# The opening of a two-layer graph-attention kernel: transfers in order of use, folds by vector, a first softmax by tile, and norms placed anew

## The chip, the cores and the metric

The kernel runs on one core of one Trainium2 chip. The core has a matrix engine (TensorE, PE in the profile), a vector engine (VectorE, DVE), an activation engine (ScalarE, ACT), a general engine (GpSimd, POOL) and a queue engine (SyncE, SP). Transfers between the chip's memory and the core's own can be issued from SP, ACT and POOL. The metric is the device time in microseconds (us) of one execution, the median of several.

## What is computed

The input x has 128 graphs of 64 nodes with 512 features each, 8192 rows of 512 numbers, all float32. One adjacency matrix of 64 x 64 serves all graphs.

```python
h = maximum(layernorm(x), 0)                        # "norm1" in the kernel
def gat(x, W, a):                                   # per head: W is [F, O], a is [2*O]
    Wh = x @ W
    f1, f2 = Wh @ a[:O], Wh @ a[O:]
    e = f1[:, None] + f2[None, :]                   # scores, 64 x 64 per graph
    e = where(e > 0, e, 0.01 * e)
    e = where(adj > 0, e, -1e9)
    return softmax(e, -1) @ Wh
h = elu(gat over 4 heads, 512 features each)        # concatenated to 2048 features
out = elu(gat(h, W_out, a_out))                     # one head
ffn = maximum(out @ w1 + b1, 0) @ w2 + b2
result = x + layernorm(ffn + out) * gamma + beta
```

## The kernel before

The 8192 rows are 64 tiles of 128 rows (two graphs each), worked in 16 groups of four tiles. The scores of the first layer don't need `x @ W`: the kernel first *folds* the vectors into the weights (`wa = W @ a`), multiplies the normalised tiles with the folded columns (`pf`), spreads these numbers into sums of pairs (`s1pe`), takes the softmax (`s1e`, `s1A`), transposes the weights of the softmax (`s1pt`, `at`), mixes the nodes (`pz`, `z`), and only then multiplies by the heads' matrices (`g_a`). Matrix products of 512 x 512 are done with seven instead of eight block products, so there are sums of blocks around them (`zs`, on DVE for the first head and on POOL later; `hS`, `h` on POOL).

Loads and the four head matrices. `nc.sync` issues from SP, `nc.scalar` from ACT, `nc.gpsimd` from POOL:

```python
    X[0] = load(0)                                  # 256 KB, from SP
    aj = const.tile([P, N], mybir.dt.int32, name="aj")
    for b in range(NB):
        nc.sync.dma_start(out=aj[ts(b, N), :], in_=adj)
    ar = ...                                        # the vectors, 8 rows of 512
    nc.sync.dma_start(out=ar, ...)
    for t in range(1, G):
        X[t] = load(t)
    ah = ...                                        # the vectors, 32 rows of 128
    nc.sync.dma_start(out=ah, ...)
    # ... (cut)
    def fetch(m):                                   # matrix m, 1 MB
        MT[m] = big.tile([P, KC, O], FP, tag=homes[m], name=f"pw{m}")
        queue = nc.scalar if m < H else nc.gpsimd
        queue.dma_start(out=MT[m], in_=mats[m].rearrange("(k p) o -> p k o", p=P))
```

The fold. Three matrices are folded on DVE: each vector is spread over the partitions by PE into a PSUM bank (`pab`, two banks for each matrix, one for each half `c` of the vector), then each of four blocks `k` of the matrix is multiplied with it and summed along the row (`jk`). The third matrix is folded on PE: transposes (`pwt`), a copy by ACT (`wT`), and products with the vectors (`pwa`).

```python
    def fold_dve(m, ab):
        for k in range(KC):
            for c in range(2):
                junk = wk.tile([P, O], FP, tag="t", name=f"jk{c}_{m}_{k}")
                nc.vector.scalar_tensor_tensor(
                    junk, MT[m][:, k, :], 1.0, ab[c], ALU.mult, ALU.mult,
                    accum_out=wa[:, k, c * H + m:c * H + m + 1],
                )
```

The norm of a tile: statistics on DVE, two steps on POOL, the activation on ACT. A tile of the third or a later group has its statistics wait for the last matrix product written down before it (`LAST["pe"]`), so that DVE doesn't wait for a late x in front of urgent work:

```python
    def norm_stats(src, tag, t):
        st = sm.tile([P, 6], FP, tag=tag + "st", name=f"{tag}st{t}")
        ins = nc.vector.bn_stats(st, src)
        if tag == "n1" and t >= 2 * G:
            tc.add_manual_dep(ins.ins, LAST["pe"].ins.name, ...)
        # ... bn_aggr, + eps on DVE (n1mv, n1ve); power -0.5 on POOL (n1rs)

    def norm1(t):
        # ... norm_stats; POOL: nb = -mean * rstd (n1nb)
        nc.scalar.activation(HN[t], X.pop(t), AF.Relu, bias=nb, scale=rstd)
        # ... POOL: sums of half tiles (hns) for two of four tiles
```

The softmax of two tiles with four heads (`q == 8`, 128 x 512 numbers):

```python
        nc.vector.tensor_tensor(e, pe, mask, ALU.add)
        # ... (f1 is not None: the second layer)
        nc.vector.scalar_tensor_tensor(e, e, ALPHA, e, ALU.mult, ALU.max)
        nc.vector.tensor_reduce(mx, e, AX.X, ALU.max)
        nc.vector.tensor_tensor(e, e, mx[:, :, None].to_broadcast([P, q, N]), ALU.subtract)
        nc.scalar.activation(e, e, AF.Exp)
        nc.vector.tensor_reduce(s, e, AX.X, ALU.add)
        nc.vector.reciprocal(r, s)
        nc.vector.tensor_tensor(A[:, :, 0:H], e, r, ALU.mult)      # shapes cut
        LAST["A"] = nc.vector.tensor_copy(A[:, :, H], A[:, :, 0])  # first head again, as a fifth
```

The opening and the first group:

```python
    for m in range(H):
        fetch(m)
    masks()                                         # small constants on DVE
    for t in range(G):
        norm1(t)
    ab = {m: spread_a(m) for m in (0, 1)}
    aT = turn_a()                                   # transposes ah (pah)
    fold_dve(0, ab[0])
    fold_dve(1, ab[1])
    fold_pe(2, aT)
    for t in range(G):
        transpose_h(t)                              # pth, copied by ACT to hT
    fold_dve(3, spread_a(3))
    for m in range(H):
        weight_sums(m, LAST["nb"])                  # POOL: sums of blocks (pt), stored (tc)
    project_f(0)                                    # pf, then L on ACT, U and R on DVE
    scores1(0)                                      # s1pe
    for p in range(2):
        attn_weights(p)                             # softmax of tiles 0 and 1, of 2 and 3
    transpose_weights(0)
    attn = attend1(0)                               # pz, copied to z by ACT and DVE
    for fn in attn[:2]:
        fn()
    head0 = project1(0, 0)                          # the first products, g_a
    # ... (cut)
        attn = attend1(g + 1) if g + 1 < NG else []
        norms, scores, turns = stage_a(g + 2)
        # ... (cut)
        first = mix(attn, tr, [nothing] * len(attn))
        # ... (cut)
        if g == 0:
            run(project2(g), first + early + norms + scores + turns + [...])
```

`run(steps, side)` writes down the steps of a product (`g_b`) and, between them, in even distance, the steps of the list `side`. `early` are the block sums of the next group.

Of the kernel before, what the change touches and what calls it, by code (L numbers as in the profile page):

```python
# [11 lines left out]
ALU = mybir.AluOpType  # L12
# [10 lines left out]
def gat_preln_kernel(  # L23
# [72 lines left out]
        return tl  # L96

    X[0] = load(0)
    aj = const.tile([P, N], mybir.dt.int32, name="aj")
    for b in range(NB):  # L100
        nc.sync.dma_start(out=aj[ts(b, N), :], in_=adj)
    ar = wk.tile([2 * H, O], FP, tag="elu", name="ar", bufs=3)
    nc.sync.dma_start(out=ar, in_=a_heads.rearrange("h (r p) -> (h r) p", p=O))
    for t in range(1, G):
        X[t] = load(t)
    ah = wk.tile([2 * H * KC, P], FP, tag="elu", name="ah", bufs=3)
    nc.sync.dma_start(out=ah, in_=a_heads.rearrange("h (r p) -> (h r) p", p=P))

    negm = const.tile([P, N], FP, name="negm")
    blkones = const.tile([P, NB, N], FP, name="blkones")  # L110
# [35 lines left out]

    def fetch(m):
        MT[m] = big.tile([P, KC, O], FP, tag=homes[m], name=f"pw{m}")
        queue = nc.scalar if m < H else nc.gpsimd
        queue.dma_start(out=MT[m], in_=mats[m].rearrange("(k p) o -> p k o", p=P))  # L150

    def spread_a(m):
# [19 lines left out]

    def fold_dve(m, ab):

        for k in range(KC):
            for c in range(2):
                junk = wk.tile([P, O], FP, tag="t", name=f"jk{c}_{m}_{k}")
                nc.vector.scalar_tensor_tensor(
                    junk, MT[m][:, k, :], 1.0, ab[c], ALU.mult, ALU.mult,
                    accum_out=wa[:, k, c * H + m:c * H + m + 1],  # L180
                )
# [69 lines left out]
    def run(steps, side=()):  # L251

        side, done = list(side), 0
        for i, fn in enumerate(steps):
            fn()
            while done * len(steps) < (i + 1) * len(side):
                side[done]()
                done += 1
# [81 lines left out]
    def norm_stats(src, tag, t):  # L340


        st = sm.tile([P, 6], FP, tag=tag + "st", name=f"{tag}st{t}")
        ins = nc.vector.bn_stats(st, src)  # L344
        if tag == "n1" and t >= 2 * G:
            tc.add_manual_dep(
                ins.ins, LAST["pe"].ins.name,
                mybir.DependencyInfo(mybir.DependencyClass.Sync, mybir.DependencyReason.DATA),
                reason="x may come late: not in front of what is urgent",
            )  # L350
        mv = sm.tile([P, 2], FP, tag=tag + "mv", name=f"{tag}mv{t}")
        nc.vector.bn_aggr(mv, st)
        ve = sm.tile([P, 1], FP, tag=tag + "ve", name=f"{tag}ve{t}")
        nc.vector.tensor_scalar(ve, mv[:, 1:2], EPS, None, ALU.add)
        rstd = sm.tile([P, 1], FP, tag=tag + "rs", name=f"{tag}rs{t}")
        nc.gpsimd.tensor_tensor(rstd, ve, mhalf, ALU.pow)
        return mv[:, 0:1], rstd
# [62 lines left out]
    def softmax(pe, f1, q, tag, t):  # L420


        w = "s1" if q == 8 else "s2"
        e = sm.tile([P, q, N], FP, tag=w + "e", name=f"{tag}e{t}", bufs=1)
        mask = negm[:, None, :].to_broadcast([P, q, N])
        if f1 is None:
            nc.vector.tensor_tensor(e, pe, mask, ALU.add)
        else:
            nc.vector.tensor_tensor(e, pe, f1[:, :, None].to_broadcast([P, q, N]), ALU.add)
            nc.vector.tensor_tensor(e, e, mask, ALU.add)  # L430
        nc.vector.scalar_tensor_tensor(e, e, ALPHA, e, ALU.mult, ALU.max)
        mx = sm.tile([P, q], FP, tag=w + "mx", name=f"{tag}mx{t}")
        nc.vector.tensor_reduce(mx, e, AX.X, ALU.max)
        nc.vector.tensor_tensor(e, e, mx[:, :, None].to_broadcast([P, q, N]), ALU.subtract)
        nc.scalar.activation(e, e, AF.Exp)
        s = sm.tile([P, q], FP, tag=w + "s", name=f"{tag}s{t}")
        nc.vector.tensor_reduce(s, e, AX.X, ALU.add)
        r = sm.tile([P, q], FP, tag=w + "r", name=f"{tag}r{t}")
        nc.vector.reciprocal(r, s)
        if q == 8:  # L440
            A = sm.tile([P, 2, H + 1, N], FP, tag=w + "A", name=f"{tag}A{t}", bufs=1)
            nc.vector.tensor_tensor(
                A[:, :, 0:H], e.rearrange("p (t h) m -> p t h m", h=H),
                r.rearrange("p (t h) -> p t h", h=H)[:, :, :, None].to_broadcast([P, 2, H, N]), ALU.mult,
            )
            LAST["A"] = nc.vector.tensor_copy(A[:, :, H], A[:, :, 0])
            return A

        rb = sm.tile([P, q, NB], FP, tag=w + "rb", name=f"{tag}rb{t}")
        nc.vector.tensor_tensor(  # L450
            rb,
            blkones[:, :, 0][:, None, :].to_broadcast([P, q, NB]),
            r[:, :, None].to_broadcast([P, q, NB]),
            ALU.mult,
        )
        A = sm.tile([P, q, NB, N], FP, tag=w + "A", name=f"{tag}A{t}", bufs=1)
        nc.vector.tensor_tensor(
            A,
            e[:, :, None, :].to_broadcast([P, q, NB, N]),
            rb[:, :, :, None].to_broadcast([P, q, NB, N]),  # L460
            ALU.mult,
        )
        return A
# [156 lines left out]
    def project2(g):  # L620
        slot = {1: "11", 2: "12", 3: "12", 4: "22", 5: "S1", 6: "11", 7: "S1"}
        h1 = dict(H1)
        wh = big.tile([P, G, FO], FP, tag="wh2", name=f"wh2_{g}")
        WH2[g] = wh

        def post(what, a, b=None, to=None):
            behind = {"s1": ("11", "S1", "11"), "s5": ("S1", "22", "11"), "c11": ("12", "12", "11")}
            if what in behind:
                dst, x0, x1 = (h1[n] for n in behind[what])
                for h in range(H):  # L630
                    nc.gpsimd.tensor_tensor(dst[:, h], x0[:, h], x1[:, h], ALU.subtract)  # L631
            if what[0] != "c":
                return
            r, c = quadrant(what)
            dst = wh[:, 2 * r:2 * r + 2, c * Q:(c + 1) * Q]
            if b is None:
                nc.scalar.copy(dst, a)  # L637
            else:
                nc.vector.tensor_tensor(dst, a, b, ALU.add)

        ms = [H + h for h in range(H)]
        return unit(
            f"b{g}", product_n(ms, lambda p, i: h1[slot[p]][:, i]), post, (1, 5, 6, 2, 7, 3, 4)
        )
# [147 lines left out]
        return [fn for _, _, fn in sorted(keyed, key=lambda k: k[:2])]  # L792


    for m in range(H):
        fetch(m)
    masks()
    for t in range(G):
# [47 lines left out]
    for g in range(NG):  # L846
        if g >= 1:
            side = stage_e(g - 1)
        else:
            side = sum(stage_a(1), [])  # L850
            for i, m in ((5, 4), (9, 5), (12, 6), (17, 7)):
                side.insert(i, lambda m=m: more_sums(m))
        done, n = 0, 6 * H
        for i in range(n):
            if i % 6 == 0:
                steps = head0 if (g, i) == (0, 0) else project1(g, i // 6)
            if (g, i // 2) != (0, 0):
                steps[i % 6]()
            while done * n < (i + 1) * len(side):
                side[done]()  # L860
                done += 1
        flush_late()
        attn = attend1(g + 1) if g + 1 < NG else []
        norms, scores, turns = stage_a(g + 2)
        tr, ff, fin = feed_forward(g - 1) if g >= 1 else ([], [], [])
        if g == NG - 1:
            run(project2(g), tr + [nothing] * 6 + ff[:2])
            run(ff[2:], [
                lambda: [scores2(g, j) for j in range(G)], lambda: spread2(g), nothing, nothing,
                lambda: softmax2(g), *[nothing] * 7, lambda: transpose_weights2(g), nothing,  # L870
                *[lambda q=q: attend2(g, q) for q in range(2)], nothing,
            ])
            continue
        early = [lambda: z_sums(g + 1, 0)]
        first = mix(attn, tr, [nothing] * len(attn))
        if g >= 1:
            first[5:5] = norms[:1]
            first[10:10] = norms[1:]
        if g == 0:
            def sums_late(m):  # L880
                fetch(m)
                weight_sums(m, LAST["A"])

            run(project2(g), first + early + norms + scores + turns + [
                load_rows, lambda: sums_late(M1), lambda: sums_late(M2)
            ])
        else:
            run(project2(g), first + mix(
                ff[:7] + early + ff[7:12] + fin[:1] + ff[12:13] + fin[1:2] + ff[13:],
                scores + [nothing] * 8,  # L890
            ) + mix(fin[2:], [nothing] + turns + [nothing] * 2))
# [32 lines left out]
```

## Time and profile before

| what | value |
|---|---|
| device time, median of 3 executions | 2320.34 us (2318.64 to 2320.38) |
| span of the profiled execution | 2318.7 us |
| granted clock of PE, mean | 0.995 of full speed |
| moved by transfers | 366.40 MB, 158 GB/s on the mean |
| start of the first head product `g_a` | 55.80 us |

In the profile a line such as `PE 2279.8 (98%)` gives the time an engine was busy, its share of the span, and the number of its instructions. PEld is PE's loading of weights, which runs beside its products. A matrix product of float32 shows as two records. A tile's name stands without its number (`pw` is any of `pw0` to `pw3`), and L158 is line 158 of the kernel. A wait is put down to the operation that came last before the waiting one started. The page's second part has the span in 40 equal slices of 58 us, one digit each, in tenths of the slice.

### The profile page before, as it was taken

Reading aid. Unit: us, or ns where it says so; the run is one execution under the profiler, and the core shown is the slowest. Engines: PE = TensorE matmul, PEld = TensorE weight load, DVE = VectorE, ACT = ScalarE, POOL = GpSimd, SP = SyncE. Lnnn points to the kernel's source line nnn. Section 1 sums busy time; section 2 is a strip of 40 time slices with the busy share of each in tenths; the row PEclk is TensorE's granted clock in tenths of the full one; section 3 lists DMA queues with packets and bytes.
Section 4 is the critical chain, followed back from the end, with each engine's and each line's share of the span. In section 5 each row is a group of like instructions: output and inputs, shape, how many; then the busy total and the mean of one; then the engine's idle time right before and its main releaser. Section 6 shows DMA issues by size and latency. Waiting matters only on the chain. (4 is left out here: it accounts for less than half of the span.)

```text
span 2318.7 us, 33446 instructions
## 1 busy us (share of the span) xinstructions
PE 2279.8 (98%) x11933; PEld 1922.7 (83%) x11933; DVE 1272.2 (55%) x2210; ACT 905.5 (39%) x1623; POOL 1029.9 (44%) x917
## 2 busy tenths in 40 slices
PE   6999999999999999999999999999999999999997
PEld 4878888888888888888888888888888888888885
DVE  6635465555646555465555646555464654744427
ACT  2534425153352534425254252533525244251512
POOL 6664544425344352444425444253443525533324
PEclk8999999999999999999999999999999999999999
DMA  8545464554545445454454545445453454635543
GB/s 296 174 171 195 133 183 135 157 161 133 183 135 176 131 147 178 133 182 132 151 171 133 182 135 162 150 140 182 132 179 131 147 180 128 182 119 168 163 146 104
DMA packets 259571, 366.40 MB, mean 158 GB/s; under 512 B 24232, under 2 KB 147144, under 8 KB 259408
## 3 DMA queue, kind: packets, MB, share of 16 engines
q1 hardware_dynamic: 252784, 343.31, 47.3%
q0 software_dynamic: 4512, 16.78, 2.0%
q10 hardware_dynamic: 2112, 4.19, 0.5%
q8 instruction: 96, 1.57, 0.3%
q14 instruction: 67, 0.55, 0.1%
HBM read 336.92 MB, written 27.26 MB: 157 GB/s over the span
## 5 line engine op out<-in xcount | busy, mean ns | idle before, releaser
L322 PE MATMUL g_b<-w,h 128*128 128x256 f32 x2560 | 592.5, 379 | 0.0
L322 PEld LDWEIGHTS g_b<-w,h 128*128 128x128 f32 x2560 | 481.4, 190 | 63.7 <-issue 0.9
L307 PE MATMUL g_a<-z,w 128*128 128x256 f32 x1520 | 360.9, 380 | 0.7 <-DVE g_a L597 0.7
L307 PE MATMUL g_a<-zs_z,w 128*128 128x256 f32 x1504 | 350.9, 381 | 0.0
L307 PEld LDWEIGHTS g_a<-zs_z,w 128*128 128x128 f32 x1504 | 282.0, 190 | 60.8 <-issue 24.3
L307 PEld LDWEIGHTS g_a<-z,w 128*128 128x128 f32 x1520 | 287.2, 190 | 45.0 <-DVE g_a L597 6.1
L601 POOL TENSOR_TENSOR hS<-hS,h 128x512 f32<-128x512 f32 x64 | 83.1, 1299 | 354.8 <-DVE hS L565 354.8
L322 PE MATMUL g_b<-w,hS 128*128 128x256 f32 x1024 | 238.5, 379 | 0.0
L563 ACT ACTIVATE exc<-g_a 128x512 f32<-128x512 f32 x256 | 152.1, 594 | 179.0 <-DVE g_a L597 106.7
L565 DVE SCALAR_TENSOR_TENSOR h<-exc,g_a 128x512 f32<-128x512 f32 x192 | 131.7, 686 | 157.3 <-ACT exc L564 156.2
L322 PEld LDWEIGHTS g_b<-w,hS 128*128 128x128 f32 x1024 | 192.1, 190 | 25.8 <-issue 1.0
L564 ACT ACTIVATE exc<-exc 128x512 f32<-128x512 f32 x256 | 161.5, 631 | 7.0
L631 POOL TENSOR_TENSOR h<-h,h 128x512 f32<-128x512 f32 x64 | 86.8, 1364 | 135.3 <-PE g_b L322 135.3
L631 POOL TENSOR_TENSOR h<-hS,h 128x512 f32<-128x512 f32 x64 | 81.2, 1270 | 142.5 <-PE g_b L322 142.5
L481 ACT COPY at<-s1pt 128x512 f32<-128x512 f32 x64 | 34.7, 588 | 279.8 <-PE s1pt L479 279.8
L332 POOL TENSOR_TENSOR zs_z<-zS,z 128x512 f32<-128x512 f32 x63 | 89.0, 1414 | 122.6 <-PE g_a L307 118.6
L773 POOL TENSOR_TENSOR xr<-xr,bs 128x512 f32<-128x512 f32 x64 | 96.1, 1502 | 72.6 <-DMA xr<-in_x_dram 58.4
L307 PE MATMUL g_c<-ot,w 128*128 128x256 f32 x512 | 122.8, 383 | 1.4 <-DVE ot L735 1.4
L322 PE MATMUL g_d<-w,rt 128*128 128x256 f32 x512 | 121.5, 380 | 2.2 <-DVE o L765 1.5
L307 PE MATMUL g_a<-zS,w 128*128 128x256 f32 x496 | 117.2, 379 | 0.0
L655 DVE SCALAR_TENSOR_TENSOR jf<-wh,ao 128x512 f32<-128x512 f32 x128 | 99.0, 811 | 31.8 <-ACT wh L637 31.6
L333 POOL TENSOR_TENSOR zs_z<-z,zs_z 128x512 f32<-128x512 f32 x63 | 85.1, 1351 | 61.8 <-PE g_a L307 39.1
(159 smaller groups left out, 3485.8 us busy)
## 6 DMA issues: line engine op xcount, KB each, us to landing
w<-tc SPq DMA_DIRECT2D x632, 256.0 KB, 2.7
w<-in_L_gnn_W_heads_dram SPq DMA_DIRECT2D x192, 256.0 KB, 3.0
w<-in_L_gnn_W_out_dram SPq DMA_DIRECT2D x192, 256.0 KB, 2.7
w<-in_L_gnn_w_dram SPq DMA_DIRECT2D x96, 256.0 KB, 2.7
x<-in_x_dram SPq DMA_DIRECT2D x64, 256.0 KB, 3.8
xr<-in_x_dram SPq DMA_DIRECT2D x128, 128.0 KB, 2.7
out_dram<-o SPq DMA_DIRECT2D x128, 128.0 KB, 2.4
tc<-pt POOLq DMA_DIRECT2D x20, 512.0 KB, 4.2
```

The source lines that it names most:

```text
L307: LAST["pe"] = nc.tensor.matmul(bk[:, o, :], w[:, k, ts(o, P)], a[:, k, :], start=start and o == 0 and k == 0, stop=k == 1, skip_group_che ...
L322: LAST["pe"] = nc.tensor.matmul(bk[:, j, :], a[:, k, ts(j, P)], w[:, k, :], start=start and k == 0 and j == 0, stop=i == len(ms) - 1 and k ...
L332: eng.tensor_tensor(s2, s1, a11, ALU.subtract)
L333: eng.tensor_tensor(s4, a12, s2, ALU.subtract)
L481: nc.scalar.copy(AT[t].rearrange("p b h n -> p (b h) n"), pt)
L563: nc.scalar.activation(ex, src, AF.Relu, scale=-1.0)
L564: nc.scalar.activation(ex, ex, AF.Exp, scale=-1.0)
L565: nc.vector.scalar_tensor_tensor(dst, ex, -1.0, src, ALU.add, ALU.max)
L601: nc.gpsimd.tensor_tensor(dst, dst, H1["22"][:, h], ALU.add)
L631: nc.gpsimd.tensor_tensor(dst[:, h], x0[:, h], x1[:, h], ALU.subtract)
L655: nc.vector.scalar_tensor_tensor(junk, WH2[g][:, j], 1.0, ao[:, c, :], ALU.mult, ALU.mult, accum_out=f[:, c, j:j + 1],)
L773: nc.gpsimd.tensor_tensor(xr, xr, bs, ALU.add)
```

## The change

It concerns the opening and the first two groups alone, and it has four parts.

1. *Transfers in order of use over three queues.* adj and `ah` go to POOL's queue; SP brings x0, `ar`, x1 to x3 and then the matrices 1 and 3; ACT brings the matrices 0 and 2 and has no more to issue. This is to have the first tiles and the third matrix early, and ACT free.
2. *Fold by vector.* The two loops of the fold change places: all four blocks with the first half of the vector, then with the second. The first bank of the vector is free sooner, and half of a fold can begin before the second half is spread.
3. *First softmax tile by tile.* The softmax of tiles 0 and 1 is done as two of 128 x 256, the second beginning after the first's subtraction. The first tile's transposes can start before the second's weights are there.
4. *Norms of the second and third group placed anew.* The statistics of the second group (`t >= G`) now wait for a matrix product too, which takes them out of the stretch before the first scores. The norms of the third group stand between the steps that mix the nodes of the second, and no more behind all of them and the next block sums.

```diff
     X[0] = load(0)
-    aj = const.tile([P, N], mybir.dt.int32, name="aj")
-    for b in range(NB):
-        nc.sync.dma_start(out=aj[ts(b, N), :], in_=adj)
     ar = wk.tile([2 * H, O], FP, tag="elu", name="ar", bufs=3)
     nc.sync.dma_start(out=ar, in_=a_heads.rearrange("h (r p) -> (h r) p", p=O))
     for t in range(1, G):
         X[t] = load(t)
     ah = wk.tile([2 * H * KC, P], FP, tag="elu", name="ah", bufs=3)
-    nc.sync.dma_start(out=ah, in_=a_heads.rearrange("h (r p) -> (h r) p", p=P))
+    nc.gpsimd.dma_start(out=ah, in_=a_heads.rearrange("h (r p) -> (h r) p", p=P))
+    aj = const.tile([P, N], mybir.dt.int32, name="aj")
+    for b in range(NB):
+        nc.gpsimd.dma_start(out=aj[ts(b, N), :], in_=adj)
 ...
-        queue = nc.scalar if m < H else nc.gpsimd
+        queue = nc.scalar if m in (0, 2) else nc.sync if m < H else nc.gpsimd
 ...
-        for k in range(KC):
-            for c in range(2):
+        for c in range(2):
+            for k in range(KC):
 ...
-        if tag == "n1" and t >= 2 * G:
+        if tag == "n1" and t >= G:
 ...
+        n = H if w == "s1" and t == 0 else q
+        for i in range(0, q, n):
+            ei, mi, si, ri = e[:, i:i + n], mx[:, i:i + n], s[:, i:i + n], r[:, i:i + n]
+            mask = negm[:, None, :].to_broadcast([P, n, N])
+            if f1 is None:
+                ins = nc.vector.tensor_tensor(ei, pe[:, i:i + n], mask, ALU.add)
+                if i:
+                    tc.add_manual_dep(ins.ins, ahead.ins.name, ...)   # one tile after the other
+            ...
+            nc.vector.scalar_tensor_tensor(ei, ei, ALPHA, ei, ALU.mult, ALU.max)
+            nc.vector.tensor_reduce(mi, ei, AX.X, ALU.max)
+            ahead = nc.vector.tensor_tensor(ei, ei, mi[:, :, None].to_broadcast([P, n, N]), ALU.subtract)
+            nc.scalar.activation(ei, ei, AF.Exp)
+            nc.vector.tensor_reduce(si, ei, AX.X, ALU.add)
+            nc.vector.reciprocal(ri, si)
+            if q == 8:
+                ...   # product and copy of the first head, for the tiles of this part
 ...
-    for m in range(H):
+    for m in (0, 2, 1, 3):
         fetch(m)
 ...
-            run(project2(g), first + early + norms + scores + turns + [
+            mixed = attn[:2] + norms[:1] + attn[2:] + norms[1:] + [nothing] * 4
+            run(project2(g), mixed + early + scores + turns + [
```

## The prediction

> **What bounds the kernel now.** I read the page first, then stretches of the span, then TensorE's waits, then the order of time. The page says that TensorE (PE) is the bound almost everywhere, and that only the first of the 40 slices is thin:
>
> ```profile
> PE 2279.8 (98%) x11933; PEld 1922.7 (83%) x11933; DVE 1272.2 (55%) x2210; ACT 905.5 (39%) x1623; POOL 1029.9 (44%) x917
> ...
> PE   6999999999999999999999999999999999999997
> ```
>
> Busy PE is not PE at its peak, but here no engine keeps it waiting in the middle, as the stretches show (busy us and instruction counts per engine, granted clock, DMA share, GB/s):
>
> ```profile
> 0.00:66.00 66.00, 46.88 (x221) 33.65 (x221) 39.64 (x113) 22.05 (x38) 36.05 (x53) 0.90 0.78 273
> 66.00:116.00 50.00, 49.74 (x282) 42.85 (x283) 32.78 (x44) 26.46 (x49) 37.60 (x34) 1.00 0.57 185
> 116.00:184.00 68.00, 64.69 (x374) 53.11 (x373) 27.47 (x52) 19.68 (x34) 44.02 (x44) 1.00 0.49 168
> 184.00:2286.00 2102.00, 2099.86 (x10979) 1778.21 (x10979) 1149.77 (x1966) 831.58 (x1492) 900.64 (x777) 1.00 0.49 155
> ```
>
> From 184 us on PE idles 2.1 us in 2102, so the change can win nothing there. It can win in the first 66 us (19.1 us idle, and a clock of 0.90 on the mean) and between 116 and 184 us (3.3 us idle). The waits of PE name the pieces; first those before 66 us, then two of the later ones (total us, times, longest):
>
> ```profile
> PE pab L158 <- DMA ar<-in_L_gnn_a_heads_dram: 8.2, 1, 8.2
> PE s1pt L479 <- DVE s1A L442: 5.4, 1, 5.4
> PE s1pe L413 <- DVE n1ve L354: 2.8, 1, 2.8
> PE pwt L189 <- DMA pw<-in_L_gnn_W_heads_dram: 2.1, 1, 2.1
> ```
>
> ```profile
> PE pth L378 <- ACT hn L366: 1.8, 2, 1.6
> ...
> PE pth L378 <- ACT hT L380: 0.8, 1, 0.8
> ```
>
> In order of time PE shows where the chain hangs (start, us, line, tile):
>
> ```profile
> 8.19 7.16 PE L158 MATMUL pab<-ar,ident 8*128 8x512 f32 x8 [8.19 <-DMA ar<-in_L_gnn_a_heads_dram]
> ...
> 17.52 3.68 PE L189 MATMUL pwt<-ident,pw 128*128 128x128 f32 x16 [2.12 <-DMA pw<-in_L_gnn_W_heads_dram]
> ...
> 30.57 2.07 PE L158 MATMUL pab<-ar,ident 8*128 8x512 f32 x2
> ```
>
> From 17.52 us, when the third weight matrix has landed, PE runs without a gap to 32.6 us: 16 transposes, four blocks of pwa, one pth, two spreads. The last spread frees VectorE (DVE) for the last seven folds, 32.68 to 37.02 us; pf ends at 37.56, then L, U and R (0.81, 0.41, 1.32 us) lead to s1pe at 40.37, the softmax to s1pt at 47.74, the mixes pz to the first product at 55.80.
>
> [...] From 8 to 10 us the two queues moved 0.43 and 0.36 MB, about even. [...]
>
> **Transfers.** Before, ACT issues all four matrices; the third issue waits for ar, the fourth for ah, so pw2 goes out near 8 us and ACT is held to 12.25 us. After, ACT issues pw0 and pw2 at once, SP brings x0, ar, x1 to x3, pw1, pw3, and adj and ah leave on POOL. Needed by the landing of pw2: x0 to x3 1.05 MB, pw0 and pw2 2.10 MB, and pw1 sharing the rest, up to 4.2 MB. At 0.375 MB/us from 2.1 us that is 13.3 us for the last byte, plus 1.2 us from last byte to landing (pw0's bytes end near 5.7 us, its landing is 0.7 + 6.2 = 6.9). Estimate 14.5 us, against 17.52. Should ar and the x's have to wait behind pw0, as adj seems to in the trace (its queue moves nothing between 3.3 and 5 us), pw2 would land near 12.9, but then pab (7.16 us from about 6.3), the pah transpose and the four hn activations hold PE to about 14.2. Either way 14.2 to 14.5.
>
> From there the built order costs PE the same: ten records of pwt 2.17, pwa 1.6, four pwt 0.87, pwa 1.65, two pwt 0.43, half a pth 0.44, pwa 1.75, half a pth 0.44, spread 2.0, pwa 1.75, a wait for the pwa copy 0.3, two pth 1.8, spread 2.07: 17.3 us. Before it was 15.1, since two pth more now stand ahead of the last spread. **Fold by vector** gives that back: the four folds with the first vector run during this time, and 4 instead of 7 remain behind the last spread, 4 x 0.607 + 0.08 = 2.5 us instead of 4.3. pf ends 20.2 us after pw2's landing, before 20.0. So the first two parts bring 3.0 us, all of it on the path.
>
> **First softmax by tile.** A 128x256 step takes 0.41 to 0.45 us on DVE and 0.42 on ACT (the second softmax has that shape), a 128x512 step 0.69 and 0.63. Counting from s1pe's end in the built order (add, leaky, max, subtract; then the second tile's steps between the first's sum, reciprocal and product), the first tile's A is ready at 4.3 us and its copied head at 5.0, the second's at 6.4 and 6.6; before both are at 5.2 and 5.5. PE starts its transposes 1.1 us sooner, waits 0.9 for the copied head and the at copy, and has the same 9.8 us of half-clock work ahead. The product then needs the z copies, whose last one on DVE now stands behind the second pair's softmax. I get 13.2 us for the first product, before 55.80 - 42.38 = 13.4: 0.2 us won. The split buys a start, not an end.
>
> **Norms of the second group.** Their four statistics leave the stretch before s1pe, where they cost nothing (U waited for L at 38.43 anyway), and now wait for the second product (60.43 us before). There DVE has h, four z copies and the sum L332 that PE waits for at 66.2 us. Four statistics at 0.65 and eight small steps at about 0.15 come in between, less the 1.7 us that DVE was idle before h; and POOL's two steps per tile (0.55 and 0.26 us) hold ACT's hn in front of the z copies. Step by step L332 starts at 66.9 instead of 65.5: 1.4 to 1.5 us **lost**.
>
> **Norms of the third group.** Before, their statistics wait for a late product at 144.4 us and POOL's n1rs stand behind six zs sums and an hS sum, until 147.6; PE then idles 1.61 + 0.22 + 0.75 us around 149.4. After, the first two stand in POOL ahead of those sums (hn ready near 136), the other two about at 148, one product before PE wants them. POOL is 3.2 us behind in other sums, which PE needs only 8 us later. 2.4 of the 2.6 us are won.
>
> **Sum.** -3.0 - 0.2 + 1.45 - 2.4 = -4.1 us; 2320.3 - 4.1 = 2316.2.
>
> **Rivals.** [...] (b) Early transfers are no gain since the even share between queues slows pw0 and pw2: if pw2 landed at 16.5, the start would win 1 us, total 2318. DMA was already at 0.9 to 1.07 of its engines from 2 us on, which speaks for it; that 1.84 MB of w pieces move behind pw3 speaks against. (c) The norms of the second group cost nothing, because PE's first sum comes late anyway: 2314.8. DVE's idle 5.5 us before h speaks for it, the wait on the second product against. (d) A burst of more: ACT free at 7 us and pw3 4 us earlier shorten more than I see: 2312.
>
> **Range and chances.** All of PE's idle time before 184 us is 19.1 + 0.3 + 3.3 = 22.7 us, 1% of the time, so a gain over 2% (46 us) isn't there to be had; a loss of that size would need PE to stall in the bulk, where the order of instructions is the same on every engine. Runs before spread over 1.7 us. Errors: pw2's landing 1.5 us, clock 1.7, norms 1; together about 3. Range 2312.0 to 2319.5. Chances 0.005, 0.99, 0.005.
>
> **What would show it.** Right: pwt starts at 14 to 15 us, pf ends near 34.6, s1pe begins near 37.4, first product near 52.7, PE waits 2 to 2.5 us for zs before its third product, and no wait on hn near 147. Wrong: pwt at 17 us or still behind pab; a granted clock back at 1.0 as late as 54 us or before 48; the third product without a wait; a new wait of PE on POOL's hS or h between 135 and 160 us.

## The result, and the profile after

The changed kernel takes 2321.49 us, the median of six executions (2318.71 to 2323.94); the kernel before, measured beside it, 2320.37 (2318.64 to 2320.67). The ratio is 1.0004, with a 95% interval of 0.9991 to 1.0017: no difference that can be measured. The prediction was 2316.2 us with a range of 2312.0 to 2319.5, so the expected gain of 4.1 us did not come: the median lies 5.3 us above the predicted one.

The page of the changed kernel, busy time of each engine and PE's share in 40 slices:

```profile
PE 2283.0 (98%) x11933; PEld 1924.5 (83%) x11933; DVE 1270.2 (55%) x2218; ACT 905.3 (39%) x1624; POOL 1030.7 (44%) x920
...
PE   7999999999999999999999999999999999999997
```

The first slice went from 6 to 7. The same stretches as before (busy us and counts of PE, PEld, DVE, ACT, POOL, then granted clock, DMA share, GB/s):

```profile
0.00:66.00 66.00, 49.35 (x221) 33.45 (x221) 41.33 (x121) 20.67 (x37) 35.67 (x53) 1.00 0.76 268
...
116.00:184.00 68.00, 65.08 (x371) 53.86 (x370) 27.47 (x52) 19.36 (x34) 43.96 (x44) 0.97 0.49 163
184.00:2286.00 2102.00, 2099.37 (x10977) 1778.49 (x10976) 1146.30 (x1965) 831.69 (x1492) 899.01 (x776) 1.00 0.50 155
```

In the first stretch PE is busy for 49.35 us, before 46.88, and has done no more: both show 221 records, and the kernel is no further at the end. Busy time that grows with the same work points to slower work. The 1.00 of its clock isn't to be believed, as the last section shows. Between 116 and 184 us PE idles 2.92 us, before 3.31, so the wait that was to go has been replaced; and the clock, before at 1.00, is at 0.97. PE's waits name the replacement (total us, times, longest):

```profile
PE pab L158 <- POOL n1rs L356: 5.9, 1, 5.9
PE s1pe L413 <- DVE R L399: 4.0, 1, 4.0
PE s1pt L493 <- DVE s1A L454: 4.0, 1, 4.0
PE pzS L553 <- ACT zS L565: 2.2, 1, 2.2
...
PE g_a L307 <- DVE zs_z L332: 1.1, 1, 1.1
PE pwt L189 <- DVE jk L178: 1.1, 1, 1.1
```

Waits at the start are shorter, as intended (pab 8.2 to 5.9, s1pt 5.4 to 4.0), and the waits of pth on hn are gone. (The view puts pab's wait down to n1rs, which happened to end last; pab reads `ar`, and in other runs, the one with the first softmax in one piece for instance, the view names the transfer of `ar`.) But s1pe waits 4.0 instead of 2.8 us, and pzS waits 2.2 us for a copy by ACT, which it did not before.

To see where the gain goes, I follow five places in both traces (us from the start of the span):

| place | before | after | lead of after | step in between |
|---|---|---|---|---|
| pf ends | 37.56 | 35.21 | 2.35 | transfers, fold |
| s1pe starts | 40.37 | 39.24 | 1.13 | L, U, R |
| first product g_a | 55.80 | 55.33 | 0.47 | softmax, pz |
| third product | 66.21 | 66.58 | -0.37 | norms of the second group |
| first product of the second group | 184.47 | 185.17 | -0.70 | norms of the third group |

From that last place to the end of the span all fourteen profiled kernels, the two and the twelve of the experiments, take between 2132.8 and 2134.3 us, before 2134.2 and after 2134.1. So between these two the rest plays no part, and each step of the table can be tried by itself.

### The profile page after: what moved, and what is told of

Its sections match the earlier page's. It is cut to its first block, busy times and chain, and to the rows that moved or that the text cites. A ratio compares the mean times of both kernels' runs of the same rounds, so it can differ in the third digit from the quotient of the medians.

```text
span 2319.3 us, 33461 instructions
## 1 busy us (share of the span) xinstructions
PE 2283.0 (98%) x11933; PEld 1924.5 (83%) x11933; DVE 1270.2 (55%) x2218; ACT 905.3 (39%) x1624; POOL 1030.7 (44%) x920
## 5 line engine op out<-in xcount | busy, mean ns | idle before, releaser
L332 POOL TENSOR_TENSOR zs_z<-zS,z 128x512 f32<-128x512 f32 x63 | 89.0, 1414 | 125.0 <-PE g_a L307 119.8
```

The costliest lines, as they stand in the source:

```text
L332: eng.tensor_tensor(s2, s1, a11, ALU.subtract)
```

## The experiments

Two theories stood against each other. Mine: each of the four parts does something in its place, but three of them move work onto another engine's critical order (R beside POOL's sums, zS behind hn, a softmax in pieces), and the sum comes out near zero. The rival: the transfers brought little, and the rest is where the clock's windows happen to fall, its stretches of half speed: the granted clock was 0.5 from 40.31 to 53.96 us in the kernel before (its 32 records of pz took 6.22 us there, where the later groups take 2.0 for 16), and from 135.79 to 139.20 us in the changed one. Times of single kernels spread over 1.6 to 5.6 us, so the places in the trace are the finer measure, though each trace is one execution: with the same opening, pf ends between 34.88 and 35.66 us in seven kernels. What holds better is the length of one stretch, compared over all kernels that share it. The times first:

| kernel | median us | ratio to before (95%) |
|---|---|---|
| norms of third group as before | 2320.43 | 1.0002 (0.9993 to 1.0010) |
| norms of second group as before | 2320.42 | 1.0001 (0.9992 to 1.0009) |
| first softmax in one piece | 2320.09 | 1.0000 (0.9992 to 1.0008) |
| transfers and fold alone | 2319.66 | 0.9998 (0.9990 to 1.0007) |
| + eight idle products | 2319.53 | 0.9996 (0.9988 to 1.0005) |
| + these and 19 in the opening | 2322.81 | 1.0014 (1.0007 to 1.0021) |
| + sums of the fourth matrix right behind R | 2321.61 | 1.0009 (1.0000 to 1.0017) |
| + third group early, hn behind the copies | 2316.90 | 0.9986 (0.9979 to 0.9993) |
| + sums of the fourth matrix behind the softmax | 2317.56 | 0.9990 (0.9982 to 0.9998) |
| joined | 2314.75 | 0.9979 (0.9971 to 0.9988) |
| joined + six idle products | 2315.06 | 0.9978 (0.9970 to 0.9986) |
| changed kernel, hn behind the copies | 2317.97 | 0.9995 (0.9987 to 1.0003) |

The lines with + stand on "transfers and fold alone".

**Norms of the third group as before**, the rest as changed:

```diff
-            mixed = attn[:2] + norms[:1] + attn[2:] + norms[1:] + [nothing] * 4
-            run(project2(g), mixed + early + scores + turns + [
+            run(project2(g), first + early + norms + scores + turns + [
```

> The changed kernel with the norms of the third group where they were (behind the block sums). Theory (their new place is an exchange of one wait for another): PE's wait for the copy zS near 134 us (2.2 us) and the slow pz behind it (3.6 us instead of 1.9) go, the wait for hn near 149 us (2.6 us in the kernel before) comes back, and the first product of the second group starts at 184.5 us, 0.6 to 0.7 earlier than the 185.17 of the changed kernel; time 1 to 2 us under the changed kernel's. Step of the prediction (the new place wins 2.4 us): product at 187.5, time 2.4 us more than the changed kernel's.

The wait for zS is gone, the waits of pth for hn are back (1.64 and 0.22 us). From the third product to the second group's first it takes 118.67 us, in the changed kernel 118.59, in the kernel before 118.26. The 185.41 us of the product miss my 184.5 and the 187.5 of the prediction's step. Part of the miss is an opening 0.45 us later at pf; part is a half-speed window of 3.41 us from 151.48 on, right behind the wait for hn, which the kernel before didn't have. The new place is an exchange, as I thought, worth a tenth of a microsecond here instead of 2.4. Over all kernels it wins nothing: 118.59, 118.98 and 119.21 us in the three with the new place and hn in front of zS, 118.25 to 118.93 in the seven with the old.

**Norms of the second group as before:**

```diff
-        if tag == "n1" and t >= G:
+        if tag == "n1" and t >= 2 * G:
```

> The changed kernel with the statistics of the second group free to run before s1pe, as before. Theory: PE's third product starts 0.6 to 1.1 us earlier after the first product (11.25 us behind it in the changed kernel, 10.4 in the kernel before), and everything behind keeps that; if the statistics now stand between U and R on DVE, s1pe itself comes up to 0.8 us later, at 39.3 to 40.0 us. Rival (the place costs nothing): third product 11.2 us behind the first.

From the first to the third product: 10.42 us, against 11.25 in the changed kernel. This is the cleanest number of the study: all four kernels whose second-group statistics wait for a product show 11.25, and all others show 10.41 or 10.42, but for the joined one with idle products (10.74). The place costs 0.83 us, so the rival, that it costs nothing, falls. s1pe came at 38.91, a little earlier than I allowed: R stood behind a statistic but ran 1.94 us instead of 2.57.

**First softmax in one piece:**

```diff
-        n = H if w == "s1" and t == 0 else q
+        n = q
```

> The changed kernel with the first softmax over both tiles at once. Theory (the half clock ends near 54.0 us whatever starts before): s1pt starts at 46.6 us instead of 45.21, without a wait for at behind it, and the first product still comes at 55.3, within 0.5 us. Rival (the split carries its start to the end): first product at 56.3 or later.

s1pt started at 46.42, the first product at 54.40. Both expectations missed: the product came neither at the same time nor later, but 0.93 us earlier than with the split. In order of time, PE of the changed kernel (start, us, line, tile):

```profile
45.21 1.09 PE L493 MATMUL s1pt<-ident,s1A 128*128 128x128 f32 x4 [3.98 <-DVE s1A L454]
46.98 1.22 PE L553 MATMUL pz<-at,hn 64*128 64x256 f32 x4 [0.67 <-ACT at L495]
48.13 1.11 PE L493 MATMUL s1pt<-ident,s1A 128*128 128x128 f32 x4
49.18 6.19 PE L553 MATMUL pz<-at,hn 64*128 64x256 f32 x28
```

and of this kernel:

```profile
46.42 1.94 PE L493 MATMUL s1pt<-ident,s1A 128*128 128x128 f32 x8 [5.38 <-DVE s1A L454]
48.29 3.93 PE L553 MATMUL pz<-at,hn 64*128 64x256 f32 x18
52.44 1.99 PE L553 MATMUL pz<-at,hn 64*128 64x256 f32 x14 [0.21 <-DVE z L567]
```

The same 8 transposes and 32 mixes take 10.12 us with the split and 7.98 without, from the first transpose to the first product; in the kernel before they took 8.06. The first four mixes alone take 1.22 us, and the other 28 almost the 6.22 us that 32 took in the kernel before. Is this the cutting or the clock? Counted from the first transpose, full speed came back after 8.66 us in the changed kernel, after 4.96 here and after 6.22 in the kernel before. Two more kernels have the split and the clock back earlier, after 6.73 us (norms of the third group as before) and 6.41 us (changed kernel, hn behind the copies): they take 9.73 and 9.57 us. So with about as much half speed as in the kernel before, the cut stretch is still 1.5 to 1.7 us longer, which is what PE's earlier start had won (1.4 us); the further 0.4 to 0.6 us of the changed kernel go with the later window. Of the cutting's part the trace names 0.67 (the wait for at); the rest is longer busy time, whose cause inside PE it doesn't name. From s1pe's end to the first product it is 13.56 and 13.72 us with the split and the early clock, 14.11 and 14.35 with the late one, and 13.35 to 13.63 in the four kernels without the split that have this stretch otherwise as before. The means are 0.4 us apart, but with the early clock the split costs only about 0.1 us on the mean.

**Transfers and fold alone** (the three edits above together):

> The kernel before with only the transfers and the order of the folds changed. Theory: pf ends near 35.2 us as in the changed kernel, s1pe starts at 39.2 to 40.0 because R on DVE runs beside the block sums of POOL (2.57 us instead of 1.32), first product at 55.3 to 55.8: of 2.35 us won at pf at most 0.5 reach the product; time 2319.5 to 2320.4. Rival (the opening carries through): s1pe near 38.0, first product near 53.4, time near 2318.

pf ends at 35.1 us, s1pe starts at 39.11, the first product at 54.72, 1.08 us ahead of before. The median is 0.78 us below that of before, whose interval holds zero. Of 2.5 us won at pf 1.26 reach s1pe and 1.0 the second group's first product. The rival (s1pe near 38.0) falls, and so does my own figure for the product, 55.3 to 55.8 us: more reached it than the 0.5 I allowed. What eats the gain stands in the order of time on DVE and POOL, in the kernel before:

```profile
38.91 1.32 DVE L399 TENSOR_TENSOR R<-U,headrow 128x512 f32<-128x512 f32 x1
```

```profile
38.41 1.26 POOL L211 TENSOR_TENSOR pt<-pw,pt 128x512 f32<-128x512 f32 x1
```

and in the changed kernel:

```profile
36.53 2.57 DVE L399 TENSOR_TENSOR R<-U,headrow 128x512 f32<-128x512 f32 x1
```

```profile
36.06 1.26 POOL L212 TENSOR_TENSOR pt<-pw 128x512 f32<-128x512 f32 x1
37.28 1.25 POOL L211 TENSOR_TENSOR pt<-pw,pt 128x512 f32<-128x512 f32 x1
38.62 1.60 POOL L219 TENSOR_TENSOR pt<-pw,pt 128x512 f32<-128x512 f32 x1
```

Before, R begins inside one POOL sum and ends 0.56 us after it. In the changed kernel it begins inside one, and ends 0.57 us after the next one is through. In the kernel of this experiment R stands behind a statistic, begins later, and takes 1.95 us; s1pe follows pf as late. The next two experiments on this are told together.

**Sums of the fourth matrix right behind R, and sums of the fourth matrix behind the softmax.** Both let R run alone; they differ in what the sums meet next. Two of the second group's statistics come behind R, two behind the first softmax, in both:

```diff
-    for m in range(H):
+    for m in range(H - 1):
         weight_sums(m, LAST["nb"])
     project_f(0)
+    weight_sums(H - 1, LAST["R"])          # first kernel
     ...
     softmax_end = LAST["A"]
+    weight_sums(H - 1, softmax_end)        # second kernel, instead
```

> The kernel with the transfers and folds of the change alone, with the block sums of the fourth matrix on POOL and the statistics of the second group put behind R. Theory (R is slow because POOL sums beside it): R takes 0.7 us instead of 1.95 and starts right behind U at 36.5, s1pe at 37.3 instead of 39.1, s1pt at 44.9, first product 1.8 us earlier, near 52.9, if the clock's windows don't fall worse. Rival (R is slow by itself, or L and not R sets s1pe): s1pe at 38.5 or later.

> The kernel with the transfers and folds of the change alone; the block sums of the fourth matrix on POOL come behind the second softmax, two of the statistics behind R, two behind the first softmax. Theory (POOL's sums and DVE's operations on two inputs from SBUF keep each other out, and before they met R, then the first softmax): with no sums beside either, R takes 0.7 us, the step s1e<-s1e 0.7 instead of the 4.1 us it took with the sums behind R, s1pe starts near 37.5, s1pt near 43.5 to 45, first product 51.5 to 53 instead of 54.7; time 1.5 to 3 us under that kernel's 2319.7. Rival (the sums are only put off and hurt as much at the sums zs on DVE before the third product): third product not earlier than 64.5.

DVE in order of time, sums right behind R:

```profile
36.76 0.69 DVE L399 TENSOR_TENSOR R<-U,headrow 128x512 f32<-128x512 f32 x1
...
40.33 4.10 DVE L446 SCALAR_TENSOR_TENSOR s1e<-s1e 128x512 f32<-128x512 f32 x1
...
45.18 1.97 DVE L448 TENSOR_TENSOR s1e<-s1e,s1mx 128x512 f32<-128x512 f32 x1
```

POOL in the same kernel:

```profile
42.61 1.25 POOL L211 TENSOR_TENSOR pt<-pw,pt 128x512 f32<-128x512 f32 x1
```

DVE with the sums behind the softmax:

```profile
36.90 0.69 DVE L399 TENSOR_TENSOR R<-U,headrow 128x512 f32<-128x512 f32 x1
...
40.02 0.69 DVE L446 SCALAR_TENSOR_TENSOR s1e<-s1e 128x512 f32<-128x512 f32 x1
...
41.47 0.69 DVE L448 TENSOR_TENSOR s1e<-s1e,s1mx 128x512 f32<-128x512 f32 x1
```

In the first, R is 0.69 us and s1pe starts at 37.59, as expected; but three POOL sums of the fourth matrix, now from 40.17 to 43.86 us, hold the step `s1e<-s1e` for 4.10 us: it ends 0.57 us after the third of them. The subtraction meets the fourth sum and takes 1.97. The start of s1pt, expected at 44.9, was at 49.65, and the kernel is 2 us slower than without the edit. In the second nothing stands beside them: s1pe at 37.74, s1pt at 44.66, first product at 52.85 and third at 63.27, all inside what the theory said; the rival wanted 64.5 for the last. 2.1 us of time are won. The stretch that R sets says it most clearly: from pf's end to s1pe's start it is 2.82 us in the kernel before, 4.02 to 4.13 in the seven kernels with the new opening, the sums in their old place and no idle products, wherever the second group's statistics stand, and 2.16 in all four with these sums moved. Of the 2.3 us by which s1pe ends earlier than with transfers and fold alone, 0.9 belong to the clock, not to R: it was full until 38.81 us, and s1pe took 1.09 us instead of 1.99. The sums don't lengthen every step beside them: in the kernel before, all 24 folds jk, which read one input from SBUF and one from a PSUM bank, took 0.676 to 0.686 us, 19 of them with a sum of POOL's beside them. The three steps of the opening that took longer, R (1.32, 1.95 and 2.57 us), s1e<-s1e (4.10) and the subtraction (1.97), have both inputs in SBUF, and each took 0.69 without a sum beside it. One of them was held for three sums in a row, 3.4 us over its 0.69.

**Idle products.** Do the slow mixes, at half speed until 52 us, hold the first product? Matrix products that serve nothing fill PE's pauses, three between pf and s1pe and five between s1pe and s1pt:

```diff
+    def warm(n, src, name):
+        b = bank(name).rearrange("p a b -> p (a b)")
+        for i in range(n):
+            ins = nc.tensor.matmul(b, ident, src, start=True, stop=True)   # cut: the first waits for the last pf / s1pe
     project_f(0)
+    warm(3, HN[0], "warm0")
     scores1(0)
+    warm(5, HN[0], "warm1")
```

> The kernel with the transfers and folds of the change alone, and eight matrix products of 128x512 that serve nothing: three between pf and s1pe, five between s1pe and s1pt. Theory (what holds the first product back is half speed, and it comes from the two pauses): s1pe takes 1.0 to 1.5 us instead of 1.99, the transposes s1pt stand 0.11 us apart instead of 0.21, and the first product starts 7.98 - 3.5 = 4.5 us behind s1pt instead of 7.98, near 50.5 us instead of 54.7; time 3 to 4 us under that kernel's 2319.7. Rival (z copies on DVE bound that stretch, or clock windows fall as they like): product at 53.5 or later, time within 1 us.

The clock was full from 36.34 us on and s1pe took 1.09 us, but the first product came only at 54.42: 6.95 us behind s1pt instead of the expected 4.5. PE now waits 0.94 us for ACT, where an hn of the second group stands in front of copies of z, and the first softmax lost 1.1 us behind a small step of the second group's norms, which waits for POOL. Time: the same within 0.2 us. The rival holds: half speed alone is not what bounds this stretch; copies and the softmax stand close behind it.

The opening is slow too: in the kernel with the eight, eight transposes pth take 1.95 us at 28.25 us and 1.04 at 66.67, 0.21 and 0.11 us apart. Does that change if PE gets more to do there? In the second of these, 19 more products of 128x256 fill the opening, ahead of pab, pwt and pth:

```diff
+    def fill(dst, n):                       # from constants, into a bank that is written anew afterwards
+        for i in range(n):
+            nc.tensor.matmul(dst, ones, ones.to_broadcast(...), start=True, stop=True)
```

> As the run with eight such products, and with 19 more of 128x256 in the opening, ahead of pab, pwt and pth, from about 1.5 us on. [...] Rival (the few products don't suffice, spacing stays 0.21): pf 1 to 4 us later, since each of the 19 costs 0.85 us at half speed where PE has no gap.

The clock did rise: full from 5.20 to 8.61, from 15.44 to 18.85 and from 25.68 to 35.92 us, and the spread pab took 1.12 us instead of 2.07. But from 8.61 to 15.44 and from 18.85 to 25.68 us it stayed at half speed, and pf, which at the end waits 1.64 us for DVE's folds, ended at 38.74 us, 2.9 later than with the eight alone. The kernel is 3.3 us slower than that one. The rival's number holds, though not its spacing: most pth did stand 0.11 us apart.

**Third group early, hn behind the copies.** In the changed kernel ACT and PE around 135 us, in order of time, ACT first:

```profile
133.34 0.81 ACT L366 ACTIVATE hn<-x,n1nb,n1rs 128x512 f32<-128x512 f32 x1 [6.57 <-POOL n1nb L364]
134.06 0.56 ACT L273 COPY s_b<-g_b 128x512 f32<-128x512 f32 x1
134.53 0.81 ACT L366 ACTIVATE hn<-x,n1nb,n1rs 128x512 f32<-128x512 f32 x1
135.25 0.57 ACT L565 COPY zS<-pzS 128x512 f32<-128x512 f32 x1
```

```profile
135.87 2.08 PE L553 MATMUL pzS<-at,hns 64*128 64x256 f32 x8 [2.21 <-ACT zS L565]
137.73 1.75 PE L553 MATMUL pz<-at,hn 64*128 64x256 f32 x8
```

ACT idles 6.57 us for the norm's small POOL steps, which stand behind POOL sums until 132.4 us, while the product pzS that it has to copy ended about 130.9 us. PE then waits 2.21 us for the bank. At 135.79 us, in this wait, the clock falls to half speed until 139.20, so pzS and pz take 3.8 us instead of 2.2. The edit leaves statistics and POOL steps early and moves hn on ACT:

```diff
+            stat = [lambda t=t: norm1a(t) for t in range(2 * G, 3 * G)]     # norm1 cut in two: statistics and POOL steps
-            mixed = attn[:2] + norms[:1] + attn[2:] + norms[1:] + [nothing] * 4
+            mixed = attn[:2] + stat[:2] + attn[2:] + stat[2:] + norms + [nothing] * 3
...
-        nc.scalar.activation(HN[t], X.pop(t), AF.Relu, bias=nb, scale=rstd)
+        ins = nc.scalar.activation(HN[t], X.pop(t), AF.Relu, bias=nb, scale=rstd)
+        if 2 * G <= t < 3 * G:
+            tc.add_manual_dep(ins.ins, LAST["z"].ins.name, ...)             # behind the last copy of z
```

> The kernel with the transfers and folds of the change alone, and the statistics and POOL steps of the third group early as in the changed kernel, but the four hn on ACT behind all copies of z. Theory (in the changed kernel hn stands in front of the copy zS that PE waits for): no wait of PE over 0.5 us for zS near 134 us and no half speed there, no wait for hn near 149, and 183.46 - 65.14 = 118.3 us between the third product and the first product of the second group become 116 us; time 2 to 2.5 us under that kernel's. Rival (PE waits elsewhere as much, for POOL's block sums for one): 118 us or more.

> The changed kernel with nothing but the four hn of the third group put behind the copies of z on ACT, their statistics and POOL steps early. Theory (hn in front of zS is what undid the third part of the change): no wait for zS over 0.5 us near 134 us, from the third product to the second group's first product 115.6 us instead of 118.6, time 2318 to 2318.5. Rival: 118 us or more, time 2321.

On top of transfers and fold alone: 115.57 us from the third product to the second group's first, against 118.32; 2316.90 us against 2319.66. In the changed kernel itself: 115.31 against 118.59; 2317.97 us against 2321.49. ACT of the changed kernel with this edit:

```profile
131.22 0.59 ACT L579 COPY zS<-pzS 128x512 f32<-128x512 f32 x1 [0.47 <-PE pzS L567]
...
135.93 0.59 ACT L579 COPY z<-pz 128x512 f32<-128x512 f32 x1 [0.28 <-PE pz L567]
136.60 1.52 ACT L374 ACTIVATE hn<-x,n1nb,n1rs 128x512 f32<-128x512 f32 x2
```

The copies run as soon as PE is through, the first two hn are ready 13 us ahead of their use at 151.48 and the last at 149.52, no wait on either is left, and no half-speed window. Both expectations held, and were a little surpassed.

**Joined, and joined with idle products.** Transfers and fold, hn behind the copies (for the second group too), and the sums behind the softmax:

> The same with the third group's norms early and its hn behind the copies of z, and the second group's hn behind the copies of z of the second tile. If the gains add: 118.3 becomes 115.6 us from the third product on, and the start gains what the run without it shows: 2314 to 2315.5 us. If not: 2316.9 as with the third group alone.

> The joined kernel with one matrix product of 128x512 that serves nothing between pf and s1pe and five between s1pe and s1pt. Theory (half speed costs what the copies of z leave open): s1pt to first product 6 to 7 us instead of 8, time 1 to 2 us under the joined kernel. Rival (the window's phase decides): the same within 0.5 us.

2314.75 us, inside the range for gains that add: 2319.66 - 2.10 - 2.76 = 2314.80. This version beats the kernel before by 0.2% (0.12 to 0.29%); its slowest execution (2315.91) is faster than the fastest of either kernel (2317.41 and 2318.71). Its stretch from 116 to 184 us has almost nothing left to win:

```profile
116.00:184.00 68.00, 67.85 (x391) 56.96 (x391) 29.72 (x54) 19.93 (x35) 44.33 (x44) 1.00 0.54 172
```

The idle products bring 0.45 us between s1pt and the first product (7.75 instead of 8.20), and nothing in time: PE now waits 1.75 us there, before 0.23. The rival's number holds again.

## Why the prediction was wrong, step by step

**Transfers and fold, -3.0.** Right in kind, by the second of its two branches: from 3.3 to 6 us the queue of SP moved 0.06 MB and that of ACT 0.95 MB, and pw2 landed near 12.4 us. The 0.375 MB/us is a rate of the trace of before: 379 GB/s from 2.5 to 5 us, 0.82 of 0.95 MB on ACT's queue, and 366 from 5 to 11 us, 1.27 MB there and 0.92 on SP's; from 3.3 to 6 us the changed kernel moved 375. pwt started at 13.02 us, earlier than the 14.2 to 14.5 predicted, since pw2 was there as soon as pab was done. But its third block then waited 1.1 us for a bank that the first folds free; DVE began these at 13.28 us, behind the statistics of x3 (11.24) and its small steps on constants. pf ended at 35.21 instead of 34.6: 2.35 us won, a size. The step that failed is the next one, "so the first two parts bring 3.0 us, all of it on the path". It carried L, U and R over at "0.81, 0.41, 1.32 us". The whole opening moved 2.35 us earlier and POOL's sums only about 1.1 (the sum pt from 35.94 to 34.84), so R met two of them where it had met one, and took 2.57. I had read the 1.32 us off the trace, and not asked what R would meet after the shift. With the sums out of the way R is 0.69, and from pf to s1pe 1.87 us less are needed.

**First softmax by tile, -0.2.** It cost 0.66 in the two traces and 0.4 on the mean of four. PE's start came 1.4 us sooner and it waited for at, both as I had it; the failed step is "the same 9.8 us of half-clock work ahead". It wasn't the same: cut in two, the stretch from the first transpose to the product grew from 8.06 to 9.57 us at least, and to 10.12 where the clock came back late. Nor do the 9.8 us fit the sum that they stand in (4.3 + 0.9 + 9.8 is 15.0, not 13.2); the 8.06 us of the trace of before would.

**Norms of the second group, +1.45.** The mechanism held: DVE's sum zs comes later and PE waits for it, 1.13 us instead of 0.71. The size is 0.83, since L332 starts at 65.81 instead of the 66.9 that I had from stepping through DVE. The "2 to 2.5 us" of wait were too many. Before and after:

```profile
65.47 0.69 DVE L332 TENSOR_TENSOR zs_z<-zS,z 128x512 f32<-128x512 f32 x1
```

```profile
65.81 0.71 DVE L332 TENSOR_TENSOR zs_z<-zS,z 128x512 f32<-128x512 f32 x1 [0.16 <-ACT zS L565]
```

**Norms of the third group, -2.4.** It cost 0.33 us. "After, the first two stand in POOL ahead of those sums (hn ready near 136)": so they do, and hn is done at 134.15 and 135.34. What failed is that I looked at POOL and at PE and left out ACT between them, where hn took its place in front of zS. With that order mended the part is worth 2.7 to 3.0 us against the old place, a little more than I gave it. I had named a new wait of PE between 135 and 160 us as a sign of being wrong, but on POOL.

**Sum.** -2.35, +1.22 (L, U, R), +0.66, +0.84, +0.33 make +0.70 at the second group's first product; the span ended 0.6 us later. Predicted were -3.0, 0, -0.2, +1.45, -2.4. Of the 4.85 us between the two sums the third group's norms have 2.73, L, U and R 1.22, the softmax 0.86 and pf 0.65; the second group gives 0.61 back.

**Rivals.** (b) gave 2318 and missed too: the transfers did bring their time, 2.35 us at pf. The clock came back at 53.87 us, in the kernel before at 53.96, although the transposes began 2.5 us sooner; "as late as 54 us" had been among the signs of being wrong. So the window took a part of the lead, 0.4 to 0.6 us by the estimate above. (c) was wrong by 0.83, and (d), 2312, by more than any of them.

**Chances.** "Within 2%" was right, for the reason given: PE's idle time before 184 us is 1% of the span. The range ended at 2319.5, 2.0 us under the measured median, as it had no room for two parts that turn over. No run shows the 1.7 us that it allows for the clock; what the runs showed there is the 0.4 to 0.6 us.

## What to carry to other kernels

Before a piece of work is moved forward, list for every engine on its way, not just the one that was waiting, what it now stands in front of; in an engine's order an early helper can become a blocker, as hn in front of zS did (2.21 us of PE's time). When one chain is shifted, whatever runs beside it does not shift with it: operations of DVE like R, with two inputs from SBUF (0.69 us alone, 1.32 to 2.57 beside POOL's sums), belong where POOL is quiet, and a sum that nobody needs soon belongs behind the critical chain, not merely behind its next link. And a part that brings nothing in the whole may be worth its full size once one order is mended, so it pays to undo and to mend parts singly.

## What the runs showed of the hardware that I had not expected

**The whole opening ran at half speed.** I had taken the clock as 0.5 only from 40.3 us, where the record of before has it so. Eight transposes of 128x128 in the changed kernel, at 27.62 us, and in the changed kernel with hn behind the copies at 151.48:

```profile
27.62 1.95 PE L378 MATMUL pth<-ident,hn 128*128 128x128 f32 x8
```

```profile
151.48 1.04 PE L392 MATMUL pth<-ident,hn 128*128 128x128 f32 x8
```

The first stand 0.213 us apart, the others 0.109. From 13.02 to 35.21 us PE was busy but for 1.1 us, yet stayed at the slow pace: busy in the profile was not enough. What ran there were transposes, spreads from 8 rows (pab) and products with 2 columns (pwa); with full products put among them the clock was full from 5.20 to 8.61, from 15.44 to 18.85 and from 25.68 to 35.92 us. Why these stretches and not the others isn't shown. Nor is the slow pace shown by the record of the granted clock: in the changed kernel it has no entry before 53.87 us, and the view prints 1.00 there.

**A half-speed window can come with a wait of only 1.6 us.** Seven of the kernels have the third group's norms in their old place and a wait of 1.6 us for hn between 144 and 152 us. Four of them fell to half speed for 3.41 us during or behind it, in which eight records of g_b took 3.18 to 3.49 us instead of 1.89, and three (the kernel before among them) did not. It cost about 0.6 us: 118.67 to 118.93 us against 118.25 to 118.32. The three with the wait for zS (2.2 to 2.6 us) all fell, and none of the four without either wait did. The waits are alike (1.61 to 1.64 us), so something else decides; what, isn't shown.

**Three of POOL's sums in a row held one step of DVE until behind the last:** 4.10 us instead of 0.69, as shown above.
